# Smaller side pieces per attention step, a later zero fill and an earlier weight load in a fused adaptive-attention and expert kernel

## The chip, the cores and the metric

One core of a Trainium2 chip runs the kernel. The metric is the device time of one execution in microseconds (us), the median over runs; lower is better. Engines are called as in the profile: PE (TensorE, the matmuls), PEld (its weight loads), DVE (VectorE), ACT (ScalarE), POOL (GpSimd) and SP (SyncE, which here issues most DMAs).

## The reference

Four sequences of 512 tokens with 256 features go through two residual blocks. Everything is float32. Cut to what matters:

```python
x = x + attn(cond_ffn(x, cond_8))            # block 1
x = x + moe(mixed_linear(x, cond_8))         # block 2

# cond_ffn: per sequence one of 8 experts (argmax of cond_8): silu(x Wu + bu) * (x Wg + bg), then Wd + bd
# attn: 16 heads of 16, one shared key/value head; softmax(q k^T / 4) v, then Wo + bo
# mixed_linear: w_b = sum_g cond_8[b, g] * (weight[g] * mask); x w_b^T + bias
# moe: 8 groups of 256 tokens, softmax router, top 2 of 8 experts, capacity 128 per group and expert;
#      gelu(x wi[e]) wo[e], weighted by the probability
```

## The kernel before

The order on every engine is written out by hand (`manual_schedule`): each engine executes the instructions in the order in which the program emits them, and an instruction that waits holds up all behind it on its engine. A DMA is issued by a queue (SP's, ACT's or POOL's), and there too a DMA that waits for an earlier one's landing holds up the ones behind it.

**Start (0 to about 103 us).** Weights and inputs are loaded by SP. A loop over b = 0, 1, 2 computes the first feed-forward (`hidden`, lines 291 to 296, and `down`, lines 268 and 272). In its last pass, b = 2, the projections of sequence 0 are interleaved: queries in two halves of the output features (`q0`, `q1`, line 325, evicted by ACT, line 327), keys with values (`k`, line 340), and the transpose of the values (`v`, line 347). Queries take a detour through DRAM: two writes into `qd` (line 331) and a read back into `q` (line 332), by which the heads come to lie 32 rows apart. Ahead of this last pass ACT issues one DMA that fills the buffer `xp` (8.7 MB) with zeros (line 362). Then come six leading steps of maxima, with the first feed-forward of sequence 3 between them.

**Attention (48 steps for b = 0 to 2, 16 for b = 3).** A step n belongs to sequence b = n // 16, place k = n % 16, and holds

- `maxima` for step n + 6: four matmuls over 32 rows (line 388), each followed by a reduce on DVE (line 392). They use 3 PSUM banks "m" in turn;
- `exponentials` for step n: four matmuls over 32 rows (line 418), each evicted by ACT's Exp (line 422), in 4 banks "x" in turn. These banks also serve the side pieces;
- `weigh` for step n − 1: matmuls of the values with the exponentials (line 436), into bank "a", copied out every fourth step (line 445) and stored to `od` (line 446);
- every fourth step `shifted`: the row maxima are transposed (line 400) and written by four small DMAs (line 404) into rows of `q`, where the exponentials three steps later read them;
- `side`: the pieces that a table names for the place k.

The table before is one list, `beside`, for b = 0, 1 and 2. A piece is (offset, name): offset 1 prepares the next sequence (`q0`, `q1`, `k`, `v`), −1 finishes the previous one (`values` and `inv` fetch the sums and outputs from `od` and give their inverse by way of `ivd`, lines 457, 461, 486, 487, 491; `norm0`, `norm1`, line 499; `out0` to `out3`, the output projection by chunks of 128 tokens, lines 516 and 521; `rT0`, `rT1`, transposes, line 537; `mix0` to `mix3`, the mixed weights, lines 548 and 552; `choose`, the router, lines 565 to 568), and −2 ranks the experts of the one before that and scatters its rows (`rank0`, `rank1`, lines 578 to 596; `places`, line 614; `rows`, lines 627 to 645; `send`, lines 651 to 663; `row0` to `row3`, POOL's scatter, line 669). `bias` (line 507) adds a bias to the residual input of the own sequence.

The order in a step depends on whether a piece has matmuls (`ON_PE`); such a step is called dense:

```python
elif dense:
    maxima(m, (0, 1)); exponentials(n, (2, 3)); side(b, k)
    maxima(m, (2, 3)); exponentials(n, (0, 1)); weigh(n - 1, (0, 1, 2, 3))
else:
    maxima(m, (0, 1)); exponentials(n, (2, 3)); weigh(n - 1, (2, 3))
    maxima(m, (2, 3)); exponentials(n, (0, 1)); side(b, k); weigh(n - 1, (0, 1))
```

(written on fewer lines here; `shifted` stands ahead of the last part). In a dense step the weighing is four matmuls of 512 columns, in the other twice four of 256.

**Experts (from about 372 us).** Units of 128 or 256 rows of one expert are worked off by `run`. For each, SP loads the up weights (`fetch_in`, line 933 by way of 940), the down weights (`fetch_out`) and the rows (`fetch_rows`, lines 952 and 955, which wait for the scatters); then `turn` (transposes, lines 995, 997), `up` (line 1068), `put` (line 1103) and a scatter that adds into the output (line 1117). The loads of units 0 and 1 are issued in steps of the last sequence by `first_pairs`.

Of the kernel before, what the change touches and what calls it, by code (L numbers as in the profile page):

```python
# [18 lines left out]
B = 4  # L19
# [23 lines left out]
def adaln_attn_ffn_kernel(  # L43
# [32 lines left out]
    def bank(tag):  # L76
        return ps.tile([P, 512], F32, tag=tag, name=f"ps_{tag}", bufs=BANKS[tag])
# [238 lines left out]
    def project(b):  # L316

        s = seqs[b]
        s["q"] = q_tiles[b % 2]

        def queries(co):
            def piece():
                pq = bank("x")
                for c in range(2):
                    mm(pq, wq_sb[:, c, ts(co, P)], coT[:, c, ts(b, T)], start=c == 0, stop=c == 1)  # L325
                qs = qp.tile([P, T], F32, name="stage", bufs=4)
                nc.scalar.activation(
                    qs, pq, AF.Identity, bias=bqs_sb[:, co : co + 1], scale=HD**-0.5
                )
                for n in range(2):  # L330
                    nc.sync.dma_start(qd[co, 0:P:2, n, :], qs[ts(n, 64), :])
                nc.sync.dma_start(s["q"][:, ts(co, 2), :], qd[co])
            return piece

        def keys():

            s["k"] = qp.tile([P, T], F32, name="k")
            pk = bank("x")
            for c in range(2):
                mm(pk, wk_sb[:, c, :], coT[:, c, ts(b, T)], start=c == 0, stop=c == 1)  # L340
            nc.scalar.activation(s["k"], pk, AF.Identity, bias=bk_sb)

        def values():
            s["v"] = v_tiles[b % 2]
            pv = bank("x")
            for sc in range(4):
                nc.tensor.transpose(pv[:, ts(sc, P)], s["k"][:, ts(sc, P)], ident)
            nc.vector.tensor_copy(
                s["v"][:, :, 0:HD].rearrange("p s (j d) -> p s j d", j=2),
                pv.rearrange("p (s j d) -> p s j d", s=4, j=4)[:, :, 0:2, 3:19:2],  # L350
            )

        return {
            "q0": queries(0), "q1": queries(1), "k": keys, "v": values,
        }

    bqs_sb = const.tile([P, 2], F32, name="bqs_sb")
    projection = {0: project(0)}
    for b in range(B - 1):
        if b == B - 2:  # L360

            nc.scalar.dma_start(
                xp.rearrange("(p r) c -> p r c", p=P),
                zeros.unsqueeze(1).to_broadcast([P, NE * EROWS // P + 2, XROW]),
            )
        for hc in range(4):
            hidden(b, hc)
            if (b, hc) > (1, 0):
                for _ in range(4):
                    if len(mixing) > NE:  # L370
                        mixed(*mixing.pop(0))
            if hc == 0 and b > 0:
                down(b - 1, 0)
                down(b - 1, 1)
            if b == B - 2:
                if hc == 0:
                    nc.vector.tensor_scalar(bqs_sb, bq_sb, HD**-0.5, None, ALU.mult)
                projection[0][("q0", "q1", "k", "v")[hc]]()
    def maxima(m, js):

        u, i = divmod(m, 4)
        b, hg = divmod(u, 4)
        q = seqs[b]["q"]
        k = seqs[b]["k"]
        nm = negm[u % 2]
        for j in js:
            pm = bank("x" if len(js) == 4 and j == 3 else "m")
            mm(  # L388
                pm, q[32 * j : 32 * j + 32, i, ts(hg, P)],
                k[32 * j : 32 * j + 32, :], start=True, stop=True,  # L390
            )
            nc.vector.tensor_reduce(  # L392
                nm[:, i, j : j + 1], pm, AX.X, ALU.max, negate=True
            )
# [318 lines left out]
    def route_mixed(b):  # L713
# [19 lines left out]

    beside = [
        [(1, "q0"), (-2, "rank0")],
        [(1, "q1"), (-2, "rank1")],
        [(-1, "values"), (1, "k"), (-2, "places"), (-2, "rows")],
        [(-2, "send")],  # L740
        [(-1, "inv"), (-2, "row0")],
        [(-2, "row1")],
        [(-1, "norm0"), (-2, "row2")],
        [(-1, "norm1"), (-2, "row3")],
        [(-1, "out0"), (-1, "out1")],
        [(-1, "out2"), (-1, "out3")],
        [(-1, "rT0"), (-1, "rT1"), (1, "v")],
        [(-1, "mix0"), (-1, "mix1")],
        [(-1, "mix2"), (-1, "mix3")],
        [(-1, "choose")],  # L750
        [(0, "bias")],
        [],
    ]
    last = [
        [(-2, "rank0")],
        [(-1, "values"), (-2, "rank1")],
# [10 lines left out]
        [(-1, "send"), (-1, "row0"), (0, "values0"), (0, "pairs3")],  # L767
        [(0, "pairs4")],
        [(0, "pairs5"), (-1, "row1")],
        [(0, "bias")],  # L770
    ]
    ON_PE = ("q", "k", "v", "out", "rT", "mix")

# [21 lines left out]
    def side(b, k):  # L795

        for f, *of in halves.get(k, ()) if b == 0 else ():
            f(*of)
            if f is down:
                mixed(*mixing.pop(0))  # L800
                mixed(*mixing.pop(0))
        for off, name in (last if b == B - 1 else beside)[k]:
            to = b + off
            if not 0 <= to < B:
                continue
            if name[:5] == "pairs":
                first_pairs(name[5:])
                continue
            if off == 1:
                if name == "q0":  # L810
                    projection[to] = project(to)
                projection[to][name]()
            else:
                work[to][name]()
# [129 lines left out]
    def fetch_out(u):  # L944
        wo_of[u] = wexp.tile([P, F // P, D], F32, name="wo2_sb")
        quarters(wo_of[u], wo2, reg[u])
# [21 lines left out]
    def first_pairs(part):  # L968
        if part == "0":
            parts.append(list_of_pairs(0, N0))  # L970
            next(parts[0])
        elif part == "1":
            next(parts[0], None)
        elif part == "2":
            fetch_in(0)
            fetch_rows(0)
            fetch_rows(1)
        elif part == "3":
            for _ in list_of_pairs(N0, NA - N0):
                pass  # L980
        elif part == "4":

            i = fetch_in(1)
            tc.add_manual_dep(i.ins, weighed[-1].ins.name, AFTER, reason="not at once")
            fetch_out(0)
        else:
            turn(0, "x")

    def turn(u, tag="a"):

# [151 lines left out]
    for n in range(STEPS + 1):  # L1142
        m = n + LEAD
        if n == 16:
# [5 lines left out]
            texp = fp.tile([P, NUNIT], F32, name="texp", bufs=1)  # L1150
            table = fp.tile([P, 2, NUNIT], I32, name="table", bufs=1)
            count = fp.tile([P, 1], I32, name="count", bufs=1)
        if n in (0, 27, 43, 56):
            residual((0, 27, 43, 56).index(n))
        b, k = divmod(n, 16)
        names = [name for _, name in (last if b == B - 1 else beside)[k]] if b < B else []
        dense = any(
            name.rstrip("0123") in ON_PE and (b > 0 or name in projection[0]) for name in names
        ) or (b == 0 and k in halves)
        if m >= STEPS:  # L1160
            if n < STEPS:
# [58 lines left out]
    def run(units, rows, begun=False):  # L1220
# [3 lines left out]
        for k in range(len(units) + 1):  # L1224
            for u in units[k : k + 1]:
                for x in rows(k):
                    fetch_rows(units[x])
                if begun and k == 1:

                    for n in (2, 3):  # L1230
                        fetch_in(units[n])
                        fetch_out(units[n - 1])
                if begun and k == 0:
                    turn(units[1], "x")
                else:
# [130 lines left out]
```

## Time and profile before

| what | value |
|---|---|
| time, median of 3 runs | 649.66 us (646.1 to 649.91) |
| the profiled execution's own time | 648.39 us |
| its span | 646.6 us |
| PE busy | 625.3 us, 97% |
| DVE, ACT, POOL busy | 334.5, 226.3, 110.9 us |
| DMA moved | 107.11 MB |
| chain that ended last | PE 89%, DMA 5% |

The page gives busy time by engine, and the span in 40 slices of 16.2 us: a digit is the busy share in tenths, and PEclk the clock that was granted to PE, in tenths of full speed. An instruction's line is that of the program. Matmul records are counted twice per float32 matmul; their busy time is the time in which at least one of them ran. Waits tell which instruction was waited for last. A group's mean is the time of one record, and since records overlap, the time that a group takes on PE is read from the timeline, from the start of one group to the start of the next.

### The profile page before, as it was taken

What the parts mean: (1) busy time and instruction counts of PE and PEld (TensorE: products, weight loads), DVE (VectorE), ACT (ScalarE), POOL (GpSimd) and SP (SyncE); (2) the same over time, 40 slices, a digit from 0 to 9 for tenths busy, and PEclk for the clock granted to TensorE, in tenths of its full rate; (3) what the DMA queues carried; (4) which work ended last, traced back from release to release, by engine and by line L of the source; (5) the groups of instructions that cost most, each with busy time, mean ns of one, the idle gap of its engine ahead of it and who ended that gap; (6) DMA issues with size and microseconds to landing.
All of it is one profiled execution on the core that took longest, in us unless ns stands there. A gap on an engine that the chain in (4) does not pass through costs nothing.

```text
span 646.6 us, 10096 instructions
## 1 busy us (share of the span) xinstructions
PE 625.3 (97%) x3704; PEld 366.0 (57%) x3704; DVE 334.5 (52%) x831; ACT 226.3 (35%) x406; POOL 110.9 (17%) x146
## 2 busy tenths in 40 slices
PE   9999899999999999999999999999999999999990
PEld 3444343334323433344335368888899999778880
DVE  1174464677658677876896754358222221322320
ACT  1212114556556455555654651221111111111220
POOL 1600000000000000310023051116332213313332
PEclk9999899999999999999999999999999999999995
DMA  7999502200042203321033288936899999888711
GB/s 238 382 272 344 172 4 76 70 2 18 18 139 63 84 18 112 106 101 49 18 104 117 82 297 243 345 98 176 267 275 329 312 339 318 244 283 259 215 20 19
DMA packets 65403, 107.11 MB, mean 166 GB/s; under 512 B 6914, under 2 KB 26946, under 8 KB 65346
## 3 DMA queue, kind: packets, MB, share of 16 engines
q1 hardware_dynamic: 50066, 87.96, 41.3%
q0 software_dynamic: 6400, 8.72, 6.8%
q10 hardware_dynamic: 8880, 9.71, 4.8%
q8 instruction: 31, 0.51, 0.3%
q14 instruction: 26, 0.21, 0.1%
HBM read 79.59 MB, written 26.65 MB: 164 GB/s over the span
## 4 chain that ended last, share of the span: by engine, by line
PE 89%; DMA 5%; issue 1%; POOL 1%; DVE 1%; ACT 1%; SPq 0%; POOLq 0%; DVEq 0%
PE ps_m L388 22%; PE ps_m L1068 15%; PE ps_x L1103 15%; PE ps_a L436 10%; PE ps_x L268 4%; PE ps_a L291 4%; PE ps_x L293 3%; PE ps_x L548 2%; PE ps_x L516 2%; PE ps_x L325 2%; DMA wi_sb<-in_wi_dram 2%; PE ps_x L418 1%; DMA qd<-stage 1%; DMA q<-qd 1%; PE ps_a L995 1%
## 5 line engine op out<-in xcount | busy, mean ns | idle before, releaser
L392 DVE TENSOR_REDUCE negm<-ps_m 128x1 f32<-128x512 f32 x250 | 160.6, 685 | 68.9 <-PE ps_x L418 51.0
L422 ACT ACTIVATE e<-ps_x 128x512 f32<-128x512 f32 x244 | 132.5, 595 | 101.9 <-PE ps_x L418 98.8
L388 PE MATMUL ps_m<-k,q 32*128 32x512 f32 x500 | 152.3, 645 | 2.5 <-DMA q<-qd 2.5
L418 PE MATMUL ps_x<-q,k 32*128 32x512 f32 x488 | 139.4, 639 | 0.0
L1068 PE MATMUL ps_m<-xT,wi_sb 128*128 128x256 f32 (+1 forms) x672 | 115.5, 330 | 1.1 <-DMA wi_sb<-in_wi_dram 1.1
L1103 PE MATMUL ps_x<-wo_sb,e 128*128 128x256 f32 x512 | 114.3, 379 | 0.0
L1068 PEld LDWEIGHTS ps_m<-xT,wi_sb 128*128 128x128 f32 x672 | 103.6, 191 | 11.5 <-issue 2.3
L1103 PEld LDWEIGHTS ps_x<-wo_sb,e 128*128 128x128 f32 x512 | 95.6, 190 | 12.6 <-issue 0.4
L1074 ACT ACTIVATE e<-ps_m 128x512 f32<-128x512 f32 x64 | 38.0, 597 | 175.9 <-PE ps_m L1068 168.6
L388 PEld LDWEIGHTS ps_m<-k,q 32*128 32x128 f32 x500 | 45.5, 184 | 69.5 <-DVE negm L392 37.8
L1117 POOL DMA_INDIRECT out_dram<-y,to_row x36 | 55.7, 1548 | 111.8 <-DMA out_dram<-y,to_row 37.7
L436 PE MATMUL ps_a<-e,v 128*32 128x256 f32 (+1 forms) x744 | 74.4, 471 | 0.5 <-ACT e L422 0.2
L436 PEld LDWEIGHTS ps_a<-e,v 128*32 128x32 f32 x744 | 14.6, 108 | 70.3 <-issue 60.3
L997 DVE COPY xT<-ps_a 128x256 f32<-128x256 f32 (+1 forms) x23 | 12.1, 528 | 81.5 <-PE ps_a L995 79.6
L1113 DVE TENSOR_SCALAR y<-ps_x,w 128x256 f32<-128x256 f32 x32 | 15.3, 482 | 58.9 <-PE ps_x L1103 58.9
L669 POOL DMA_INDIRECT xp<-x,to_i x32 | 32.8, 1026 | 59.2 <-DVE negm L392 14.7
L418 PEld LDWEIGHTS ps_x<-q,k 32*128 32x128 f32 x488 | 38.4, 182 | 0.4 <-DVE x L521 0.2
L296 DVE SCALAR_TENSOR_TENSOR hid<-ps_x,wo_sb,sg 128x512 f32<-128x512 f32 x16 | 12.0, 749 | 43.8 <-PE ps_x L293 41.9
L291 PE MATMUL ps_a<-xT_sb,wi_sb 128*128 128x512 f32 x64 | 31.3, 611 | 0.0
L293 PE MATMUL ps_x<-xT_sb,wi_sb 128*128 128x512 f32 x64 | 30.1, 592 | 0.0
L268 PE MATMUL ps_x<-hid,wo_sb 128*128 128x512 f32 (+1 forms) x80 | 29.4, 515 | 0.0
L295 ACT ACTIVATE sg<-ps_a,wo_sb 128x512 f32<-128x512 f32 x16 | 11.0, 687 | 51.4 <-PE ps_a L291 43.8
(166 smaller groups left out, 454.3 us busy)
## 6 DMA issues: line engine op xcount, KB each, us to landing
wi_sb<-in_wi_dram SPq DMA_DIRECT2D x25, 1024.0 KB
wo_sb<-in_wo_dram SPq DMA_DIRECT2D x25, 1024.0 KB
xp<-zeros ACTq DMA_DIRECT2D x1, 8712.0 KB
q<-qd SPq DMA_DIRECT2D x8, 512.0 KB
wi_sb<-in_wcond_dram SPq DMA_DIRECT2D x15, 256.0 KB
od<-stage SPq DMA_DIRECT2D x15, 256.0 KB
xt<-xp SPq DMA_DIRECT2D x11, 264.0 KB
wo_sb<-in_wcond_dram SPq DMA_DIRECT2D x4, 517.0 KB
```

Source lines behind the costliest of these rows:

```text
L268: mm(po, wd[:, hc, ts(dc, P)], hid_of[b][:, hc, ds(t0, n)], start=hc == 0, stop=hc == 3,)
L291: mm(pu, wu[:, c, :], xT_sb[:, c, ts(b, T)], start=c == 0, stop=c == 1)
L293: mm(pg, wg[:, c, :], xT_sb[:, c, ts(b, T)], start=c == 0, stop=c == 1)
L388: mm(pm, q[32 * j : 32 * j + 32, i, ts(hg, P)], k[32 * j : 32 * j + 32, :], start=True, stop=True,)
L392: nc.vector.tensor_reduce(nm[:, i, j : j + 1], pm, AX.X, ALU.max, negate=True)
L418: mm(px, k[rows_j, ts(sc, P)], seqs[u // 4]["q"][rows_j, :, ts(u % 4, P)], start=True, stop=True,)
L422: nc.scalar.activation(e_of[n][:, :, j, :].rearrange("p h (i t) -> p i h t", i=4), px.rearrange("p (i h t) -> p i h t", i=4, h=4), AF.Exp,)
L436: i = mm(pa_of[u][32 * hh : 32 * hh + 32, j0 * P : (j0 + nj) * P], seqs[b]["v"][:, sc, :], e[:, hh, j0 : j0 + nj].rearrange("p j n -> p (j ...
L1068: i = mm(ph[:, ts(k, n)], wi_of[u][:, c, ts(f0 + k, P)], xT_of[u][:, c, :], start=c == 0, stop=c == 1,)
L1074: nc.scalar.activation(hT_of[u][:, f0 : f0 + each].rearrange("p f t -> p (f t)"), ph, AF.Gelu_apprx_tanh,)
L1103: mm(po[:, 0:D], hT_of[u][:, fc, ts(h, P)], wo_of[u][:, fc, :], start=fc == 0, stop=fc == F // P - 1,)
L1117: i = nc.gpsimd.indirect_dma_start(out=out_rows, out_offset=bass.IndirectOffsetOnAxis(ap=to, axis=0), in_=y, in_offset=None, compute_op=AL ...
```

## The change

1. **Projections by halves of tokens.** `queries` and `keys` take an argument: with half "a" or "b" they work on 256 tokens instead of 512. Both halves of the queries fill one `stage` tile; the DMAs through `qd` are issued with the second half.
2. **A table per sequence.** `beside` becomes three lists. For b = 0 it holds only the next sequence's projections, one half per step. For b = 1 and 2 it begins with `queries_first` (projections by halves, then one chunk of the output projection per step), followed by the mixed weights, one chunk per step for b = 1 and two for b = 2. `values` moves from place 2 to 1, `inv` from 4 to 3, the norms from 6 and 7 to 5 and 6. For b = 2 the pieces of offset −2 stand at places 0 to 8, with `choose` of sequence 0 ahead of them.
3. **Zeros.** The fill of `xp` is issued after the loop over b, no longer ahead of its last pass.
4. **Weights.** The up weights of unit 2 are fetched in the last step of attention, not in `run`.
5. The residual inputs are loaded at steps 28 and 44, before at 27 and 43.

```diff
-        def queries(co):
+        def queries(co, half=None):
             def piece():
-                pq = bank("x")
+                at, n = tokens(half)
+                pq = bank("x")[:, 0:n]
                 for c in range(2):
-                    mm(pq, wq_sb[:, c, ts(co, P)], coT[:, c, ts(b, T)], start=c == 0, stop=c == 1)
-                qs = qp.tile([P, T], F32, name="stage", bufs=4)
+                    mm(
+                        pq, wq_sb[:, c, ts(co, P)], coT[:, c, ds(b * T + at.start, n)],
+                        start=c == 0, stop=c == 1,
+                    )
+                if half in (None, "a"):
+                    s["qs"] = qp.tile([P, T], F32, name="stage", bufs=4)
+                qs = s["qs"]
                 nc.scalar.activation(
-                    qs, pq, AF.Identity, bias=bqs_sb[:, co : co + 1], scale=HD**-0.5
+                    qs[:, at], pq, AF.Identity, bias=bqs_sb[:, co : co + 1], scale=HD**-0.5
                 )
+                if half == "a":
+                    return
                 for n in range(2):
                     nc.sync.dma_start(qd[co, 0:P:2, n, :], qs[ts(n, 64), :])
                 nc.sync.dma_start(s["q"][:, ts(co, 2), :], qd[co])
...
     for b in range(B - 1):
-        if b == B - 2:
-
-            nc.scalar.dma_start(
-                xp.rearrange("(p r) c -> p r c", p=P),
-                zeros.unsqueeze(1).to_broadcast([P, NE * EROWS // P + 2, XROW]),
-            )
         for hc in range(4):
             hidden(b, hc)
...
+    nc.scalar.dma_start(
+        xp.rearrange("(p r) c -> p r c", p=P),
+        zeros.unsqueeze(1).to_broadcast([P, NE * EROWS // P + 2, XROW]),
+    )
+
     def maxima(m, js):
...
-    beside = [
-        [(1, "q0"), (-2, "rank0")],
-        [(1, "q1"), (-2, "rank1")],
-        [(-1, "values"), (1, "k"), (-2, "places"), (-2, "rows")],
-        [(-2, "send")],
-        [(-1, "inv"), (-2, "row0")],
-        [(-2, "row1")],
-        [(-1, "norm0"), (-2, "row2")],
-        [(-1, "norm1"), (-2, "row3")],
-        [(-1, "out0"), (-1, "out1")],
-        [(-1, "out2"), (-1, "out3")],
-        [(-1, "rT0"), (-1, "rT1"), (1, "v")],
-        [(-1, "mix0"), (-1, "mix1")],
-        [(-1, "mix2"), (-1, "mix3")],
-        [(-1, "choose")],
-        [(0, "bias")],
+    queries_first = [
+        [(1, "q0a")], [(1, "q0b"), (-1, "values")], [(1, "q1a")], [(1, "q1b"), (-1, "inv")],
+        [(1, "ka")], [(1, "kb"), (-1, "norm0")], [(1, "v"), (-1, "norm1")], [(-1, "out0")],
+        [(-1, "out1")], [(-1, "out2")], [(-1, "out3")], [(-1, "rT0"), (-1, "rT1")],
+    ]
+
+    beside = [[(1, "q0a")], [(1, "q0b")], [(1, "q1a")], [(1, "q1b")], [], [(1, "ka")], []]
+    beside += [[(1, "kb")], [], [], [(1, "v")], [], [], [], [(0, "bias")], []]
+    beside = [beside]
+    beside.append(queries_first + [
+        [(-1, "mix0")], [(-1, "mix1")], [(-1, "mix2"), (0, "bias")], [(-1, "mix3")],
+    ])
+    beside.append(queries_first + [
+        [(-1, "mix0"), (-1, "mix1")], [(-1, "mix2"), (-1, "mix3")], [(-1, "choose"), (0, "bias")],
         [],
-    ]
+    ])
+    for k, name in enumerate(
+        ("choose", "rank0", "rank1", "rows", "send", "row0", "row1", "row2", "row3")
+    ):
+        beside[2][k] = beside[2][k] + [(-2, name)]
+    beside[2][3].insert(-1, (-2, "places"))
...
-        [(0, "bias")],
+        [(0, "bias"), (0, "pairs6")],
     ]
...
             fetch_out(0)
+        elif part == "5":
+            turn(0, "x")
         else:
-            turn(0, "x")
+            i = fetch_in(2)
+            tc.add_manual_dep(i.ins, weighed[-1].ins.name, AFTER, reason="not at once")
...
-        if n in (0, 27, 43, 56):
-            residual((0, 27, 43, 56).index(n))
+        if n in (0, 28, 44, 56):
+            residual((0, 28, 44, 56).index(n))
...
-                    for n in (2, 3):
-                        fetch_in(units[n])
-                        fetch_out(units[n - 1])
+                    fetch_out(units[1])
+                    fetch_in(units[3])
+                    fetch_out(units[2])
```

`keys` is halved in the same way as `queries`. Besides the dense steps that the table makes, four steps of b = 0 are dense because halves of `down` stand in them, and two because of the mixed weights' transposes; these are not changed.

## The prediction

> **What bounds the kernel now.** I read the page first, then the waits of the PE alone, then stretches and the timeline around each place the change touches.
>
> ```profile
> span 646.6 us, 10096 instructions
> PE 625.3 (97%) x3704; PEld 366.0 (57%) x3704; DVE 334.5 (52%) x831; ACT 226.3 (35%) x406; POOL 110.9 (17%) x146
> ...
>
> ```
>
> The PE is busy for 97% of the span, so time is won only by giving it less to stream, by removing its idle gaps, or by keeping its clock up. The fifth slice of the clock (64 to 80 us) is the only one below 9 before the tail. The waits of PE name two gaps worth having:
>
> ```profile
> PE ps_m L388 <- DMA q<-qd: 2.5, 1, 2.5
> ...
> PE ps_m L1068 <- DMA wi_sb<-in_wi_dram: 1.1, 1, 1.1
> ```
>
> The first lies at 68 to 70.4 us. Stretches there (columns: PE, PEld, DVE, ACT, POOL, then granted clock, DMA share, GB/s):
>
> ```profile
> 64.00:67.00 3.00, 3.00 (x9) 1.33 (x8) 2.21 (x3) 1.37 (x2) 0.00 (x0) 1.00 1.09 342
> 67.00:70.40 3.40, 0.98 (x6) 0.45 (x4) 0.88 (x2) 0.00 (x0) 0.00 (x0) 1.00 1.03 367
> 70.40:72.00 1.60, 1.56 (x8) 0.52 (x8) 0.00 (x0) 0.00 (x0) 0.00 (x0) 0.50 0.15 49
> 72.00:74.00 2.00, 2.00 (x6) 0.84 (x3) 1.46 (x3) 0.00 (x0) 0.00 (x0) 0.54 0.07 18
> ```
>
> DMA is saturated until 70.4 us, the PE waits, and it comes back at half clock. Then two kinds of attention step, from the PE timeline: step 17 with a side piece (start, duration), and step 30 without one.
>
> ```profile
> 179.04 0.70 PE L388 MATMUL ps_m<-k,q 32*128 32x512 f32 x2
> ...
> 180.11 1.98 PE L325 MATMUL ps_x<-coT,wq_sb 128*128 128x512 f32 x4
> 182.03 0.70 PE L388 MATMUL ps_m<-k,q 32*128 32x512 f32 x2
> ...
> 183.10 1.06 PE L436 MATMUL ps_a<-e,v 128*32 128x512 f32 x8
> 184.09 0.70 PE L388 MATMUL ps_m<-k,q 32*128 32x512 f32 x2
> ...
> 236.18 0.70 PE L388 MATMUL ps_m<-k,q 32*128 32x512 f32 x2
> ...
> 237.25 0.64 PE L436 MATMUL ps_a<-e,v 128*32 128x256 f32 x8
> 237.82 0.96 PE L388 MATMUL ps_m<-k,q 32*128 32x512 f32 x2
> ...
> 239.15 0.64 PE L436 MATMUL ps_a<-e,v 128*32 128x256 f32 x8
> 239.72 0.70 PE L388 MATMUL ps_m<-k,q 32*128 32x512 f32 x2
> ```
>
> Step 17 (dense order) lasts 179.04 to 184.09 = 5.05 us: 1.07 + 1.92 side + 1.07 + 0.99 weighing, so 3.13 besides the side piece. Step 30 (other order) lasts 3.54: 1.07 + 0.57 + 1.33 + 0.57. Its second maxima take 1.33 and not 1.07: a reduce takes 0.685 (L392) and the next maxima wait for its bank, with only a 0.57 weighing between. In the dense order the side piece and the 0.99 weighing cover that. An empty step thus wastes 0.4 us.
>
> **Zeros.** Before, ACT issues the 8.7 MB fill at 40.2 us; q0's writes (issued 54.6) and its read (63.0 to 70.4) run against it. After, it stands on ACT's queue behind the silu of the third sequence's last hidden chunk, which ends at 66.6 us. Without the fill, q0 goes as in step 32: write at 247.50, read issued at 250.57, 3.1 us. So read issue at 57.7; even with the old 7.4 us it lands by 65.1, and PE needs it at 68.0. Removed: 2.46 us of idle, and the slow clock: first maxima 70.44 to 72.46 = 2.02 against 1.07 for the next (77.62 to 78.69), first L291 2.48 against 1.83 (78.69 to 80.52): 0.95 + 0.65 = 1.60. Together 4.06. The fill now runs about 66.6 to 92 (26 us at 343 GB/s, an estimate from the saturated stretches). In it falls only the first batch of row maxima, L404, at 93.12 before, about 89 after; step 0's exponentials need them at about 99. At the 7.4 us of the contended read they still land at 98.9, just in time. If they don't, the cost is the excess and, past 2.5 us, the clock again. I take 4.06; bounds 0 and 4.1.
>
> Clock: the row shows half clock after 2.46 us of idle. The Trainium skill (TensorE: Matmul & The Clock Gate, What's actually happening) says that a cold state follows at least one idle window of about 3.4 us. By that page alone this gap would cost its idle only, and the sum would be 1.6 us smaller.
>
> **Weights.** The third unit's up weights (1 MB) were issued at 391.07 behind the row fetches that wait for the scatters, and landed at 401.1; PE idled 1.05 us. Now they go out in step 63, after the weighing at 376.2 to 377.2, behind the second unit's weights and the first's down weights in one ring; 378 to 384 us already move 380 to 397 GB/s, so the scatters of 382 to 386 may finish up to 1 MB/390 = 2.7 us later, still before the transposes at 392.7 need rows fetched after them at 388.75 + about 2. I take 1.05; bounds −1.5 and 1.05.
>
> **Attention steps 0 to 47.** By the order of `beside`, dense steps go from 10+8+8 to 13+16+14. The PE's columns stay equal; what changes is packing. A side group of 8 records of 256 columns (L516) takes 1.92, but its pure rate (L1103, 3.45 per 16) is 1.71: 0.21 goes into each change between 32-row and full-array matmuls. So a half piece costs 0.85 + 0.21 = 1.07 (an estimate) and its step 3.13 + 1.07 = 4.20. Formerly a pair of one full and one empty step cost 5.06 + 3.54 = 8.60; now 2 × 4.20 = 8.40. Gain 0.20 per pair; pairs: 3 (b = 0), 3 + 2 + 2 (b = 1), 3 + 2 (b = 2) = 15, 3.0 us.
>
> The Trainium skill (TensorEngine Tiling (Array Packing), Key Properties) speaks against the change: changing the tiling mode drains the array. It names no price; with 0.32 per change instead of 0.21 the pairs would gain nothing.
>
> The rest, by DVE: v leaves the transposes' step and joins norm1: formerly 4.96 + 3.91, now 4.3 + 4.1, 0.45 in each of b = 1, 2: 0.9. In b = 2 the empty steps 35, 36, 38 took 4.08, 4.16, 3.79 (rows, send, norm0), 1.4 over 3.54; dense steps absorb send and norm0. But the rank and row chains, formerly covered by 1.92 us of PE work, stand beside 1.07: rank0 is 8 operations in 1.78 (246.06 to 247.84), after two reduces at +2.4, so the third reduce ends at +4.83 and PE waits 0.7; the rows (2.1) and the reciprocal (0.54) in one step: 1.1; choice and bias (1.22) in one empty step: 0.3. Net −0.7. Bias in b = 1 keeps its 0.4 behind the last reduces. Halved evictions on ACT (two of 0.47 for one of 0.69, L272) are hidden: 2.38 + 0.47 of 4.2 us; without that cover they would cost 9 × 0.25 = 2.3. Together 3.2.
>
> **SP's queue** is what the moves load most. Before, in b = 2:
>
> ```profile
> 252.55 1.09 SPq L331 DMA_DIRECT2D qd<-stage  x2
> 255.88 0.33 SPq L332 DMA_DIRECT2D q<-qd  x1
> 256.31 2.44 SPq L404 DMA_DIRECT2D q<-nmT  x4
> 258.80 0.56 SPq L457 DMA_DIRECT2D sum<-od  x1
> ```
>
> q<-qd waits for its writes, and all behind it waits too. After, sum and o (1.8 us) stand in front of the maxima rows. From step 17's side piece: q write +1.7, read +5, sum and o to +7.4, rows issued to +9.9, landed by +11.9 (in step 57 rows issued by 366.0 served a matmul at 367.97, so at most 2.0 us). Step 20 needs them at 3.13 + 2 × 4.20 = +11.5: up to 0.4 late in b = 1; b = 2 has its DVE waits as slack. The second read likewise stands before the inverse: q1b at +10.1, read issued +13.4, ivd +13.8, inv +15.3, landing 2 to 4 later; norm0 wants it at +18.05: 0 to 1.2 late. I take −0.4 for both. Attention: 2.8; bounds −2 (all nine evictions uncovered, 2.3, and both waits in both batches, 3.2, against 3.2) and 5 (the DVE chains hidden too).
>
> **Sum.** 4.06 + 1.05 + 2.8 = 7.9 us. The profiled execution took 648.39 (span 646.6 and 1.8 around it): 640.5. The median shown is 649.66, 1.3 higher; by it 641.8. I say 641.0.
>
> **Rivals.** (1) Zeros and weights pay, the steps don't: drains, DVE chains and late rows eat the 2.8. Gain 5.1, 644.0 between the two bases. For it: 0.20 per pair is thin, b = 2 is nearly paced by DVE. Against: every term is a row or two rows' difference. (2) The fill's new place stalls step 0: the maxima rows land late by what q0 lost, and the 4.06 are given back there. Gain 3.9, 645.0. For it: small transfers took 7 to 8 us beside the fill. Against: about 10 us of lead. That the fill isn't moved past what it hurts I exclude: on ACT's queue it now follows an instruction that ends 1.5 us after q0 has landed at the latest. (3) Slower: one mechanism, SP's wait for q's writes in steps 17, 19, 33, 35. If they take the contended 7.9 us instead of 3.1, rows come 4.8 + 0.4 late and the inverse about as late; each such gap also halves the clock (1.6): about 12.5 per batch, 25 in two, 666. It turns the sign from writes of about 5 us on (four gaps of 2 us take the whole 7.9). Against: the four writes there took 3.07 to 3.57, with the fill long done.
>
> **Chances.** Forecast 0.62, (1) 0.19, (2) 0.12, (3) 0.07. Measurement tells about 1% from no change, 6.5 us: faster below 643.2. The forecast's own spread crosses it upward sometimes, (1) and (2) lie mostly inside: faster 0.65, same 0.29, slower 0.06. Range 636 to 646.5: below, attention at its bound of 5 and 3 us of run spread (646.1 to 649.91 shown); above, the rivals (1) and (2).
>
> **What would show it.** Right: no PE wait on q<-qd at 68 us and clock 1.00 to 80 us; no wait on wi_sb near 400; steps 16 to 31 in about 67.7 us instead of 69.7, 32 to 47 in about 70.7 instead of 71.4, with waits on L392 in the rank0 and rows steps. Wrong: PE waits on L404's or inv's transfers in steps 20, 21, 36, 37; a late step 0; half-piece steps above 4.4 us.

## The result: no gain, and where the forecast 8 us went

| | median (lowest to highest), us | ratio to before, 95% interval |
|---|---|---|
| before, same chip | 647.25 (643.89 to 649.91), 12 runs | |
| after | 648.74 (642.83 to 651.85), 12 runs | 1.0026 [1.0002, 1.0050] |

Forecast were 641.0 us and a range of 636 to 646.5. The change made the kernel neither faster nor slower by 1%. The profiled execution of after is the longest of its twelve (651.85 us, span 650.1), 3.1 us above the median, so its trace shows the losses larger than the median does.

The page of after, first lines and the clock:

```profile
span 650.1 us, 9895 instructions
PE 627.6 (97%) x3604; PEld 366.4 (56%) x3604; DVE 333.9 (51%) x831; ACT 227.5 (35%) x415; POOL 111.3 (17%) x146
...
PEclk9999999999999999899999998999999999999996
```

The clock of before, to compare:

```profile
PEclk9999899999999999999999999999999999999995
```

The slow fifth slice of before is gone; two others (the 17th, 260 to 276 us, and the 25th, 390 to 406) have come in its place. PE's waits name them (engine, tile and line that waited, what released it, us in total, times, longest):

```profile
PE ps_a L1023 <- DMA xt<-xp: 3.0, 1, 3.0
PE ps_x L93 <- DVE nil L91: 1.5, 1, 1.5
PE ps_m L410 <- DVE negm L414: 1.4, 2, 1.0
PE ps_x L440 <- DMA q<-nmT: 0.5, 1, 0.5
```

The two waits of before, on q<-qd and on wi_sb, are no longer there. Three new ones are: the token rows of the expert phase (xt), the row maxima (negm) twice, the maxima's rows (nmT). The same places in both traces, by the start of PE's side piece in steps 0, 16 and 32, of the first and of the third unit's up matmuls:

| stretch | before | after | after minus before |
|---|---|---|---|
| start to step 0 | 104.23 | 100.63 | −3.60 |
| steps 0 to 15 | 70.83 | 69.93 | −0.90 |
| steps 16 to 31 | 69.70 | 70.78 | +1.08 |
| step 32 to first expert matmul | 132.44 | 135.95 | +3.51 |
| to the third unit's up matmuls | 24.06 | 27.72 | +3.66 |
| rest of the span | 245.34 | 245.09 | −0.25 |

The sum is +3.5 us, as the spans say.

**The zeros' place worked.** The stretches that showed a wait and the half clock before (PE, PEld, DVE, ACT, POOL, then granted clock, DMA share, GB/s):

```profile
64.00:67.00 3.00, 3.00 (x8) 1.33 (x7) 2.70 (x4) 1.23 (x2) 0.00 (x0) 1.00 0.50 178
67.00:70.40 3.40, 3.40 (x17) 1.49 (x16) 1.68 (x4) 0.15 (x1) 0.00 (x0) 1.00 0.76 262
70.40:72.00 1.60, 1.60 (x5) 0.76 (x4) 1.60 (x3) 0.46 (x1) 0.00 (x0) 1.00 1.05 359
72.00:74.00 2.00, 2.00 (x11) 1.13 (x9) 0.77 (x2) 0.54 (x2) 0.00 (x0) 1.00 1.08 343
```

PE is busy throughout and the clock stays at 1.00. The first projection began 0.54 us later in this execution (52.47 for 51.93), so the gain is 3.60 + 0.54 = 4.1.

**A half piece costs what was estimated.** Steps 18 and 19 and the start of step 20 on PE (start, duration):

```profile
177.89 0.70 PE L410 MATMUL ps_m<-k,q 32*128 32x512 f32 x2
...
178.96 1.13 PE L331 MATMUL ps_x<-coT,wq_sb 128*128 128x256 f32 x4
180.02 0.70 PE L410 MATMUL ps_m<-k,q 32*128 32x512 f32 x2
...
182.09 0.70 PE L410 MATMUL ps_m<-k,q 32*128 32x512 f32 x2
...
186.29 1.13 PE L410 MATMUL ps_m<-k,q 32*128 32x512 f32 x4
187.95 1.13 PE L440 MATMUL ps_x<-q,k 32*128 32x512 f32 x4 [0.54 <-DMA q<-nmT]
```

177.89 to 182.09 and on to 186.29 are 4.20 us each; the side piece takes 180.02 − 178.96 = 1.06. Then step 20 begins with all four maxima alone. The exponentials' scores (L440), which in other steps run beside the maxima in other rows of the array (in step 18 they begin at 177.90), wait for the maxima's rows and come 1.66 us after them: the wait is 0.54, but the step takes 5.85 (186.29 to 192.14), 1.65 more than its neighbours, since the overlap is lost too.

**SP's queue.** The lines of step 32 and after, as shown of before:

```profile
250.27 0.33 SPq L345 DMA_DIRECT2D q<-qd  x1
...
252.69 2.36 SPq L426 DMA_DIRECT2D q<-nmT  x4
256.15 1.16 SPq L344 DMA_DIRECT2D qd<-stage  x2
259.15 0.32 SPq L345 DMA_DIRECT2D q<-qd  x1
259.57 0.38 SPq L509 DMA_DIRECT2D ivd<-iv  x1
263.14 1.33 SPq L513 DMA_DIRECT2D inv<-ivd  x2
```

The second chunk's write takes 3.00 us until its read leaves, as forecast. But the inverse's own write and read come right behind that 512 KB read: from ivd to inv 3.57 us (3.29 in step 19), where 1.45 were measured in a run without it in front (below), and 1.45 and 1.50 in before. On DVE that is

```profile
264.49 1.29 DVE L414 TENSOR_REDUCE negm<-ps_m 128x1 f32<-128x512 f32 x2 [0.78 <-PE ps_x L440]
268.10 1.02 DVE L521 TENSOR_TENSOR attn<-o,inv 128x512 f32<-128x512 f32 x1 [2.32 <-DMA inv<-ivd]
268.97 1.26 DVE L414 TENSOR_REDUCE negm<-ps_m 128x1 f32<-128x512 f32 x2
```

inv is first used 268.10 − 263.14 = 5.0 us after its issue. DVE's queue is in order: the normalisation waits, the reduces behind it too, and PE waits 1.04 us for them at 268.65. From 269.95 to 276.78 the granted clock is 0.50. Step 38 takes 8.90 us (267.53 to 276.43).

**The transition.** PE at the first down matmuls:

```profile
395.93 0.86 PE L1023 MATMUL ps_a<-ident,xt 128*128 128x128 f32 x4 [2.97 <-DMA xt<-xp]
396.58 5.79 PE L1131 MATMUL ps_x<-wo_sb,e 128*128 128x256 f32 x19
```

and the stretches there, before's next to after's:

```profile
384.00:388.00 4.00, 4.00 (x21) 3.51 (x20) 2.53 (x1) 1.41 (x3) 2.45 (x3) 1.00 0.57 214
388.00:392.00 4.00, 4.00 (x20) 3.54 (x19) 0.00 (x0) 1.49 (x3) 0.00 (x0) 1.00 0.49 98
```

```profile
384.00:388.00 4.00, 4.00 (x20) 3.54 (x19) 2.62 (x1) 1.32 (x3) 2.54 (x3) 1.00 1.06 395
388.00:392.00 4.00, 4.00 (x20) 3.51 (x20) 0.00 (x0) 1.44 (x3) 0.00 (x0) 1.00 0.41 92
...
396.00:398.00 2.00, 2.00 (x8) 1.73 (x9) 1.11 (x4) 0.00 (x0) 0.00 (x0) 0.56 1.07 243
```

With one megabyte more, the DMA engines are full until 388 us. The last scatter was issued at 386.1 and 386.2, but the row fetch, which waits for the scatters to land, leaves at 390.12 instead of 388.75. It is two transfers, the second 1.2 us behind the first. In before the first was issued 0.83 us ahead of the two transfers that ACT issues for the last sequence's values (inv<-od at 389.58, o<-od at 390.85); in after inv<-od leaves first, at 389.70, and o<-od, at 390.94, stands between the two halves of the fetch. In after both queues begin to move data in the same microsecond (q1 is SP's queue, q10 ACT's; packets, MB, share of the DMA engines from 391 to 392):

```profile
q1 hardware_dynamic: 28, 0.03, 54.0%
q10 hardware_dynamic: 33, 0.07, 35.5%
```

PE can use the rows only 5.8 us after their issue. The clock in the stretch behind the wait is 0.56, 0.50 from 396.25 to 399.66.

### The profile page after: what moved, and what is told of

Read it like the earlier page. It is cut to its first block, busy times and chain, and to the rows that moved or that the text cites. A ratio compares the mean times of both kernels' runs of the same rounds, so it can differ in the third digit from the quotient of the medians.

```text
span 650.1 us, 9895 instructions
## 1 busy us (share of the span) xinstructions
PE 627.6 (97%) x3604; PEld 366.4 (56%) x3604; DVE 333.9 (51%) x831; ACT 227.5 (35%) x415; POOL 111.3 (17%) x146
## 4 chain that ended last, share of the span: by engine, by line
PE 88%; DMA 4%; issue 2%; DVE 2%; POOL 1%; ACT 0%; SPq 0%; POOLq 0%; DVEq 0%
PE ps_m L410 19%; PE ps_x L1131 17%; PE ps_m L1096 15%; PE ps_a L458 8%; PE ps_x L268 4%; PE ps_a L291 4%; PE ps_x L293 4%; PE ps_x L570 2%; PE ps_x L538 2%; PE ps_x L331 2%; DMA inv<-ivd 1%; PE ps_x L440 1%; PE ps_a L1023 1%; DMA ivd<-iv 1%; PE ps_x L93 1%
## 5 line engine op out<-in xcount | busy, mean ns | idle before, releaser
L440 PE MATMUL ps_x<-q,k 32*128 32x512 f32 x488 | 141.5, 647 | 0.5 <-DMA q<-nmT 0.5
L1131 PE MATMUL ps_x<-wo_sb,e 128*128 128x256 f32 x512 | 115.8, 383 | 0.0
L410 PEld LDWEIGHTS ps_m<-k,q 32*128 32x128 f32 x500 | 42.2, 184 | 72.8 <-DVE negm L414 52.1
L458 PE MATMUL ps_a<-e,v 128*32 128x512 f32 (+1 forms) x608 | 71.6, 543 | 0.5 <-ACT e L444 0.2
L1141 DVE TENSOR_SCALAR y<-ps_x,w 128x256 f32<-128x256 f32 x32 | 15.3, 482 | 60.3 <-PE ps_x L1131 60.3
L458 PEld LDWEIGHTS ps_a<-e,v 128*32 128x32 f32 x608 | 12.0, 108 | 58.0 <-issue 51.1
L440 PEld LDWEIGHTS ps_x<-q,k 32*128 32x128 f32 x488 | 38.7, 184 | 2.2 <-issue 1.3
```

The source lines that it names most:

```text
L410: mm(pm, q[32 * j : 32 * j + 32, i, ts(hg, P)], k[32 * j : 32 * j + 32, :], start=True, stop=True,)
L440: mm(px, k[rows_j, ts(sc, P)], seqs[u // 4]["q"][rows_j, :, ts(u % 4, P)], start=True, stop=True,)
L458: i = mm(pa_of[u][32 * hh : 32 * hh + 32, j0 * P : (j0 + nj) * P], seqs[b]["v"][:, sc, :], e[:, hh, j0 : j0 + nj].rearrange("p j n -> p (j ...
L1131: mm(po[:, 0:D], hT_of[u][:, fc, ts(h, P)], wo_of[u][:, fc, :], start=fc == 0, stop=fc == F // P - 1,)
```

## Experiments

Ten kernels. Each was compared with before on the same chip, and before stood at 647.2 us in the first four, 647.3 in the next four, 646.9 in the last two. The theory: the zeros and the half pieces pay as forecast; the rest is lost in two places, SP's queue in steps 17 to 22 and 33 to 38, and the row fetch of the transition. The rivals: the half pieces themselves don't pay, or the new place of the fill costs something later.

**Weights put back.** After, with the third unit's up weights asked for where before asks for them.

```
-        [(0, "bias"), (0, "pairs6")],
+        [(0, "bias")],
...
-                    fetch_out(units[1])
-                    fetch_in(units[3])
-                    fetch_out(units[2])
+                    for n in (2, 3):
+                        fetch_in(units[n])
+                        fetch_out(units[n - 1])
```

> The changed kernel with the up weights of unit 2 fetched in the expert loop again, as before the change; all else as changed. Theory (late transfers): the early 1 MB fetch holds up the last scatters' landing, so the row fetch of unit 2 goes out 1.4 us later, behind the last sequence's inverse on ACT's queue, and PE waits 3.0 us at 393 and runs at half clock for 1.6 more. Undone, the wait on xt<-xp is gone, a wait of about 1 us on wi_sb near 400 is back, and the span falls by about 3.5 us against the changed kernel (650.1 to about 646.5). Rival (the rows are late for another reason, such as ACT's inverse alone): the wait stays and the span falls by less than 1 us.

Measured: 643.88 us, ratio 0.9946 [0.9929, 0.9962], 4.9 below after. The wait on xt is gone, one of 0.9 on wi_sb is back. In the two traces, which are 8.1 us apart, 3.78 us of the gain lie between the first and the third unit's up matmuls (23.94 for 27.72), about what was expected. Another 4.3 lie ahead of them, from step 32 on (131.69 for 135.95), since step 38 was milder here: DVE waited 1.21 us for inv instead of 2.32, PE not at all, and the clock stayed at 1.00. The edit acts only at 377 us and can't have done that; so a part of the 4.9 isn't the weights'.

**Queries sent late.** After, where in the second and third sequence's steps the write and the read of both query chunks are issued behind the inverse (steps 20 and 22, 36 and 38) and not with their projection. In the table `q0bb` is `q0b` without these transfers and `q0d` the transfers alone.

```
-        [(1, "q0a")], [(1, "q0b"), (-1, "values")], [(1, "q1a")], [(1, "q1b"), (-1, "inv")],
-        [(1, "ka")], [(1, "kb"), (-1, "norm0")], [(1, "v"), (-1, "norm1")], [(-1, "out0")],
+        [(1, "q0a")], [(1, "q0bb"), (-1, "values")], [(1, "q1a")], [(1, "q1bb"), (-1, "inv")],
+        [(1, "ka"), (1, "q0d")], [(1, "kb"), (-1, "norm0")],
+        [(1, "v"), (-1, "norm1"), (1, "q1d")], [(-1, "out0")],
```

> The changed kernel, but for sequences 1 and 2 the queries' writes to DRAM and their read back are issued two to three steps later (steps 4 and 6 of a sequence, behind the fetch of the inverse), the matmuls unchanged. Theory (late transfers on SP): the two reads that wait for their writes no longer stand ahead of the maxima rows and of the inverse; PE's wait on q<-nmT in step 20 (1.65 us longer step) and DVE's waits on inv<-ivd in steps 21 and 37 (1.7 and 2.3 us, with half clock after the second) go; steps 16 to 31 take 68.0 us instead of 70.7 and steps 32 to 47 about 71 instead of 75.7; span about 7 us lower than the changed kernel, 643. Rival (the inverse is late because of DMA traffic or its own chain, not its place in the queue): DVE still waits over 1 us for inv in both sequences and the span falls by less than 3 us. Rival (the half pieces themselves cost: drains): steps stay above 4.4 us.

Measured: 643.61 us, ratio 0.9953 [0.9934, 0.9972]. No wait on negm, nmT or inv is left, steps 16 to 31 take 67.85 us (after 70.78), and from ivd to inv it is 1.45 us. What remains is 2.9 on xt.

**Both.** After with both edits.

> Both edits of the two runs before together: the queries sent late and the weights fetched as before the change. Theory: the gains add, about 10.5 us under the changed kernel's span of 650.1, so 639.5, and about 7 us under the kernel before, faster by 1.1%. If the rest of the span is paced by something else (the rival), it lands at 644 or above.

Measured: 640.51 us, ratio 0.9886 [0.9869, 0.9903]: faster than before and after. That this is also the forecast's 641.0 is luck: the forecast counted from a before that was 1.1 to 2.4 us slower than the 647.25 measured with after, and its 1.05 for the weights isn't in this kernel. PE's only wait above 0.2 us, beside one of 1.5 at the start that every kernel here has, is 0.7 on wi_sb.

**Zeros only.** Before, with the fill moved as in after and nothing else.

```
-        if b == B - 2:
-
-            nc.scalar.dma_start(
-                xp.rearrange("(p r) c -> p r c", p=P),
...
+    nc.scalar.dma_start(
+        xp.rearrange("(p r) c -> p r c", p=P),
```

> The kernel before with one edit: the zero fill issued after the loop, as in the changed kernel. Theory: PE's wait of 2.46 us at 68 us and the half clock behind it (1.6) go, nothing else moves: span 4.1 us lower, 642.5, time about 0.6% lower. Rival (the fill meets the first maxima rows or the residual load instead): no gain, with a wait in step 0.

Measured: 643.65 us, ratio 0.9937 [0.9921, 0.9954]. With the three before it every term can be read as a difference of medians: zeros 647.19 − 643.65 = 3.5; steps with SP's queue out of the way, 643.65 − 640.51 = 3.1; SP's queue, 643.88 − 640.51 = 3.4 lost; weights, 643.61 − 640.51 = 3.1 lost. They add up to 3.5 + 3.1 − 3.4 − 3.1 = 0.1, while after was 1.5 slower than before: together the two losses cost some 1.7 more than one by one. In the 3.1 of the steps stand the halves, the table and the residual loads' new steps; these were not tested apart. PE's wait on wi_sb, 1.1 in before, is 1.6 here, which takes a part of the 4.1 that the zeros gave at step 0. The rival that the half pieces don't pay falls, and so does the fill's place.

**Weights only.** Before, with the third unit's up weights asked for in the last attention step (the first experiment's edit the other way round).

> The kernel before with one part of the change alone: the third unit's up weights (1 MB) asked for in the last attention step instead of behind the scatters. Before is at 647.2 us. Theory (one megabyte more in the transfers at 378 to 388 us holds the scatters and so the row fetch of the next units back; the matmul that needs the rows waits about 3 us and comes back at half clock; from the two kernels that differ in this part alone, 643.6 with it and 640.5 without): about 3 us slower, 650.3, with a wait of PE on xt of 2.5 to 3.0 us and none on wi_sb. Rival (the rows were late only because of the change's other parts): the forecast's 1.05 us gained, 646.1, no wait on xt.

Measured: 650.58 us, ratio 1.0054 [1.0034, 1.0075], 3.3 slower.

```profile
PE ps_a L998 <- DMA xt<-xp: 3.3, 1, 3.3
PE ps_m L388 <- DMA q<-qd: 2.9, 1, 2.9
```

The second line is the old wait of the zeros, which this kernel keeps. The wait on wi_sb is gone and 3.3 us on xt stand in its place: the weights' move by itself makes the kernel slower, with nothing else of the change in it.

**Inverse first.** Weights put back, and in steps 19 and 35 only the order of two entries swapped, so that the inverse's transfers leave ahead of the second chunk's.

```
-[(1, "q1b"), (-1, "inv")]
+[(-1, "inv"), (1, "q1b")]
```

> The changed kernel with the weights put back, and in steps 19 and 35 the inverse's two transfers issued ahead of the second query chunk's write and read instead of behind them; the maxima's rows stay behind the first chunk's. Without the swap 643.9 us, with all of the queries' transfers out of the way 640.5. Theory (both waits cost: the late rows 1.65 us in step 20, the late inverse about 1.1 in step 22 and some 0.5 in step 38): 642.3, the waits of DVE on inv gone (from 2.0 and 1.2 us), step 20 still near 5.8 us. Rival 1 (the rows are all of it): 643.9. Rival 2 (the inverse is all of it): 640.6, step 20 at 4.2.

Measured: 641.81 us, ratio 0.9934 [0.9899, 0.9968]. The waits on inv are gone, step 20 still takes 5.45 us (186.14 to 191.59) although PE stands idle for no more than 0.14 in it, steps 16 to 31 take 69.06 (70.96 without the swap, 67.86 with both chunks out of the way).

**First chunk sent late.** The complement: weights put back, only the first chunk's transfers moved behind the inverse.

> The complement of the swap: the changed kernel with the weights put back, and for the second and third sequences only the first query chunk's write and read moved behind the inverse (step 20 and 36); the second chunk's stay where the change has them. Theory (both waits cost): step 20 at 4.2 us, the waits of DVE on inv still 1 to 2 us, 642.2. Rival 1 (the rows are all of it): 640.6. Rival 2 (the inverse is all of it): 643.9.

Measured: 645.64 us, ratio 0.9978 [0.9960, 0.9995]: 1.8 slower than with both chunks early. That was nobody's forecast. DVE and PE in step 22:

```profile
195.22 1.02 DVE L534 TENSOR_TENSOR attn<-o,inv 128x512 f32<-128x512 f32 x1 [2.53 <-DMA inv<-ivd]
```

```profile
196.81 0.69 PE L423 MATMUL ps_m<-k,q 32*128 32x512 f32 x1 [1.25 <-DVE negm L427]
```

```profile
196.00:198.00 2.00, 1.19 (x6) 0.31 (x6) 1.97 (x5) 0.00 (x0) 0.00 (x0) 0.92 0.14 53
198.00:200.00 2.00, 2.00 (x11) 1.23 (x12) 1.71 (x4) 1.09 (x2) 0.00 (x0) 0.50 0.73 125
```

Step 20 is on time, so PE begins step 22 at 194.44 (196.05 with both chunks early); the inverse is used at 195.22 (196.33), only 1.1 us sooner. The wait that the late rows had covered now stands open: 2.53 us on DVE (2.02 with both early), 1.25 on PE (0.74), and half clock behind it. The two waits don't add; the first hides a part of the second, and removing the first alone uncovers it, here 0.5 us on either engine. What made it dearer than the 1.4 us won in step 20 is the half clock, which the trace of the kernel with both early does not have. In the traces steps 16 to 31 are 0.45 us longer (71.41 for 70.96) and the span 1.0; the rest of the 1.8 isn't shown.

**Second unit's weights earlier.** Queries sent late, third unit's weights early as in after, and the second unit's up weights asked for with the first's.

```
             fetch_rows(0)
             fetch_rows(1)
+            fetch_in(1)
...
-            i = fetch_in(1)
-            tc.add_manual_dep(i.ins, weighed[-1].ins.name, AFTER, reason="not at once")
```

> The kernel with all queries' transfers behind the inverse (643.6 us) and the third unit's up weights still early, but the second unit's up weights (1 MB) asked for about 7 us sooner, next to the first's, where the transfers have room. Theory (it is the volume in front of the scatters that made the rows late): PE's wait on xt falls from 2.9 us to under 1, no half clock behind it, about 640.3, and no wait on wi_sb. Rival 1 (the rows are late because the third unit's weights stand before them in the queue at all): wait 2.9 as before, 643.6. Rival 2 (the earlier megabyte holds up the last attention steps' own small transfers): new PE waits at 360 to 368 us, slower than 643.6.

Measured: 647.03 us, ratio 1.0000 [0.9984, 1.0015], worse than without it: PE waits 5.1 us for xt. There was no room where I had thought: the DMA share is 0.76 at 360 to 364 us and 1.01 to 1.06 from 364 to 380. A megabyte moved within a full stretch doesn't end it sooner. Why the rows came another microsecond later (issued 4.1 us after the last scatter's issue ended, against 3.1) stays open.

**Half the weights early.** Queries sent late, half of the third unit's up weights early and half late.

```
-            i = fetch_in(2)
+            i = fetch_in(2, 0)
...
+                    fetch_in(units[2], 1)
                     fetch_out(units[1])
```

Part 0 takes the first two of the four quarters, part 1 the other two.

> All queries' transfers behind the inverse, and of the third unit's up weights only half (0.5 MB) asked for in the last attention step, the other half behind the row fetch as before. With the whole of it early 643.6 us, with none 640.5. Theory (a threshold: the row fetch is late for good once it is issued behind ACT's two transfers inv<-od and o<-od, which leave at a fixed point of PE's work; half a megabyte delays it by some 0.7 us, and it was 0.9 ahead of them): the rows still leave ahead, no PE wait on xt, no half clock, the wait on wi_sb (0.7) gone, 640.0. Rival (every byte counts alike): a wait on xt of about 1.5 us, 642.

Measured: 638.56 us, ratio 0.9882 [0.9862, 0.9902]. No wait on xt, none on wi_sb, the clock at 9 in all of the page's slices but the last. The rows are issued at 381.34, 0.12 us behind ACT's first transfer and ahead of its second, and are used at 384.46 without a wait of PE. The theory wanted them issued ahead of both; they are ahead where data moves, for from 382 to 383 us SP's queue is alone:

```profile
q1 hardware_dynamic: 103, 0.11, 56.0%
```

So from the first up matmul to the third unit's it takes 23.67 us with no megabyte early, 23.11 with half, 27.69 with a whole one: not a price per byte. It is the fastest kernel here; that it beats the one without early weights isn't shown. The two intervals overlap, and of the 2.0 us between the medians the traces put 0.56 here, while the profiled run without early weights also lost time to half clock at 160 us (below).

**Values later.** Queries sent late, the whole megabyte early, but ACT's inv<-od and o<-od issued two activations later.

```
-        0: ["-row2", "-row3", "inv0"], 2: ["values1"], 4: ["inv1", "norm0", "norm1"],
+        0: ["-row2", "-row3", "inv0"], 3: ["values1"], 4: ["inv1", "norm0", "norm1"],
```

> All queries' transfers behind the inverse and the whole of the third unit's up weights early (643.6 us, PE waits 2.9 us for xt), but ACT's two transfers inv<-od and o<-od issued two activations later (some 3 us), so that the row fetch leaves ahead of them. Theory (the place behind these two is most of the lateness: the fetch took 5.6 us from issue to the matmul, against at most 3.8 where it was ahead): issue at 382.0 as before, wait on xt at most 1.1 us, clock above 0.9 behind it, about 641. Rival 1 (the megabyte alone): wait still 2.5 to 3, 643.6. Rival 2 (the last inverse becomes late instead): a new wait of PE on attn's writer near 397 us, 643 to 645.

Measured: 644.40 us, ratio 0.9960 [0.9946, 0.9975].

```profile
PE ps_x L551 <- DVE attn L534: 2.7, 2, 2.1
PE ps_x L93 <- DVE nil L91: 1.5, 1, 1.5
PE ps_a L1037 <- DMA xt<-xp: 0.5, 1, 0.5
```

The rows leave at 382.84, no sooner than before the edit (381.96), and are used 2.7 us later instead of 5.6: the place behind ACT's transfers was the larger part of their lateness, the theory's point. Its time was missed, for the second rival came true as well: the last inverse is late now, PE waits 2.7 us for attn, and half clock follows (0.50 from 399.94 to 403.35).

The DMA packets of the traces show this place best: when the rows' first packet starts, when ACT's does, and how long it takes until the 256th packet of the rows starts.

| kernel | rows' first packet | ACT's first packet | rows' first 256 packets, us | PE's wait on xt, us |
|---|---|---|---|---|
| before | 389.76 | 391.05 | 1.5 | none |
| both undone | 383.28 | 385.17 | 1.2 | none |
| half early | 382.36 | 383.29 | 1.4 | none |
| values later | 383.86 | 388.97 | 1.2 | 0.5 |
| queries sent late | 383.12 | 382.92 | 3.3 | 2.9 |
| after | 391.40 | 391.20 | 3.3 | 3.0 |
| weights only | 392.08 | 391.34 | 3.2 | 3.3 |
| second unit's weights earlier | 384.81 | 383.40 | 2.4 | 5.1 |

Where the rows start first they move in 1.2 to 1.5 us, where ACT's start first in 2.4 to 3.3. The longest wait goes with the fetch that was also issued latest, 8.9 us behind the second group of up matmuls (after 7.7, queries sent late 7.8).

## Why the prediction was wrong

By its own terms, with the differences of medians from the experiments (both undone is the kernel with both edits):

| term of the sum | forecast, us gained | measured |
|---|---|---|
| zeros | 4.06 | 3.5 (4.1 in the trace) |
| attention steps | 3.2 | 3.1 |
| SP's queue | −0.4 | −3.4 with the weights put back, −5.1 within the change (about −8.0 in the profiled execution) |
| weights | 1.05 | −3.3 alone, −3.1 with the queries sent late, −4.9 within the change |

3.5 + 3.1 − 3.4 − 4.9 = −1.7: after was measured 1.5 slower (648.74 against 647.25). The sum comes out by construction. The last two terms don't separate cleanly: −5.1 for the queue goes with −3.1 for the weights, −3.4 with −4.9, and no run says which of the two the 1.8 us between belong to.

**Zeros and steps: right.** The fill, its half clock and the half-piece step of 4.20 us are as worked out. That the steps' total fits so well is partly luck: steps 0 to 15 gained 0.9 us for the 0.6 of three pairs, and from the kernel with only the zeros moved to the one with both undone steps 16 to 31 gained 1.8 for 2.0 and steps 32 to 47 0.4 for 0.7. The maxima's rows beside the moved fill came in time: PE has no wait in step 0. The doubt that more changes of tiling mode (between 32-row and full-array matmuls) would eat the pairs' gain is settled by the 4.20.

**SP's queue: the failed term in steps 16 to 47.** The place was nearly right (steps 20, 21, 36, 37 were named; PE lost the time in 20, 22 and 38) and the size wrong by a factor of eight or more in the medians. Three assumptions failed. First, "ivd +13.8, inv +15.3": 1.5 us from ivd to inv, where 3.3 and 3.6 were measured behind the 512 KB read. Second, "landing 2 to 4 later": it was 4.3 in step 19 (issued 191.90, used 196.24) and 5.0 in step 35. The Trainium skill (DMA: Bandwidth & Descriptors, Queues, rings and completion order) says that on each DMA engine one issuer's descriptors (the pieces of a transfer) are taken in the order of its ring (the list of them); the runs agree for the time from ivd to inv: 1.45 us where SP had issued nothing for 4 us, 2.39 a microsecond behind the maxima's rows, 3.57 with the read directly in front. Third, a late transfer was priced as its lateness. In step 20 0.54 us of wait cost 1.65, since the exponentials had lost the maxima they run beside; in step 38 1.04 us of PE's wait were followed by 6.8 us of half clock, some 3 lost by an estimate. Profiled, the parts are 1.65 in step 20, and 1.4 in step 22 and 4.9 in step 38 beyond the 3.96 us that both take with the queries sent late: 8.0 in all. The rival that gave 666 had the right places and the wrong cause: the queries' writes took 3.0 to 3.4 us, about as forecast; the transfers behind their read were late.

**Weights: the failed term in the transition.** "The scatters may finish up to 2.7 us later, still before the transposes need rows fetched after them at 388.75 + about 2." The fetch left 1.4 later, inside that bound. The "about 2" was wrong: the rows took 5.8 us, since their packets now started behind ACT's, of two transfers of 256 KB each, which leave at a point fixed by PE's progress (inv<-od 7.2 to 7.3 us after the second group of up matmuls in before and after). I had counted the queue that the weights are put on, not the order in which another queue's transfers would then stand. The lower bound of −1.5 left out the clock.

**The interval.** The range ended at 646.5 to hold its first two rivals, and in both of them the weights pay. Both failed terms were bounded by lateness alone. The bound given for attention (−2) held the steps and SP's queue together in the medians, 3.1 − 3.4 = −0.3 or, just, 3.1 − 5.1 = −2.0; the weights' bound of −1.5 didn't hold −3.1.

## What to carry to other kernels

When work is moved so that an in-order queue issues a large transfer sooner, list the small transfers right behind it and give them the latency they show behind a large one, not the one they show alone; the remedy here was to issue the large one later, since nobody needed it soon. A prefetch that filled the last idle of the DMA engines wasn't free here, though its bytes fit: ask which dependent transfer leaves next, and behind whom. Test two suspected waits one by one and together: here the removal of one alone was slower than none.

## What was not expected of the hardware

**Half clock after some waits and not after others.** After 0.5 us of PE idle (row fetch in the last experiment) the clock stayed at 1.00; after 1.04 and 1.25 us (steps 38 and 22 above) it was 0.50, for 6.8 and 3.4 us; yet in the kernel with only the zeros moved PE waited 1.6 us for wi_sb, and the stretch behind it reads

```profile
397.00:399.00 2.00, 1.97 (x9) 1.80 (x10) 0.80 (x2) 0.00 (x0) 0.43 (x1) 1.00 1.08 347
```

at full clock. And it fell where PE is shown busy all the time, in the kernel with both parts undone, behind 16 matmul records of eight columns each (157.6 to 159.5 us; the same matmuls in the other runs were followed by full clock):

```profile
158.00:159.00 1.00, 1.00 (x11) 1.00 (x11) 1.00 (x3) 0.86 (x2) 0.00 (x0) 1.00 0.70 262
...
160.00:161.00 1.00, 1.00 (x8) 0.00 (x0) 0.00 (x0) 0.00 (x0) 0.00 (x0) 0.50 0.00 0
161.00:162.00 1.00, 1.00 (x8) 0.20 (x8) 0.73 (x2) 0.65 (x2) 0.00 (x0) 0.50 0.00 0
162.00:163.00 1.00, 1.00 (x8) 0.00 (x0) 0.87 (x2) 0.44 (x1) 0.00 (x0) 0.50 0.00 0
```

The Trainium skill (TensorE: Matmul & The Clock Gate, What's actually happening) describes a free-running window of about 3.4 us whose phase differs from run to run. That a gap's price varies agrees with it; that a gap of 1.04 us was enough does not agree with a whole idle window. No run here tells what share of a window decides. The stretches of half clock in the traces lasted 3.4 us or, in step 38 and in the kernel with the second unit's weights earlier, 6.8. So a wait of one to three microseconds had a price between zero and about 3.4 us beside itself (an estimate: half of 6.8). It would fit that kernels with such waits scatter: after ran from 642.8 to 651.9, the kernel with both parts undone, in which PE waits no more than 0.7 us behind the start, from 639.4 to 641.3. That the clock makes this scatter isn't shown.

**A small transfer behind a large one.** The same 32 KB write (ivd) took 1.45, 2.4 or 3.2 to 3.6 us until the read of it could leave, going with what its own queue had issued in the microseconds before it.
